# Macaron layer on one core: the last batch's scores in another order, first products drawn ahead, and the tile pools resized to make room

## The chip, the core and the metric

The kernel runs on one core of a Trainium2 chip. The metric is device time in microseconds (us). Its engines, as they are named here: PE (TensorE; PEld is its weight loading), DVE (VectorE), ACT (ScalarE), POOL (GpSimd) and SP (SyncE, which here only issues transfers). Each runs its own instructions in order, and they wait for each other by semaphores.

## The reference

`x` is 16 batches of 256 tokens of width 256, in float32. Three residual stages follow each other:

```
x = x + 0.5 * ffn(layernorm(x), w1, b1, w2, b2)     # w1, w2 quantised to -1, 0, 1
x = x + attn(layernorm(x), Wq, Wk, Wv, Wo)
x = x + 0.5 * ffn(layernorm(x), w1, b1, w2, b2)
# ffn:  gelu(x @ w1q.T + b1) @ w2q.T + b2, width 1024
# attn: 16 heads of 16, rotary embedding, causal softmax(q k / 4) v, then Wo
```

## The kernel before, in words

All 4096 tokens stay on the chip (`xs`, 8 tiles of 4 x 128 tokens). The two feed-forwards go over 8 blocks of 512 tokens, the attention over 16 batches of 256. Every instruction goes through the class `InOrder` (line 167, the line that the profile shows for nearly all of them), so each engine's order is the order of the Python calls.

**Feed-forward** (`ffn`, from line 273). A block's tokens are normalised into `xn` (`prepare`, line 282; one buffer), turned by PE and copied by ACT into `xnT` (`turn_in`, line 291; a high part and, by DVE's subtraction, a rest). `step(u)` (line 366) does for its block `i` and chunk `f` of 128 hidden columns: `up`, four PE products of 128x512 into a PSUM tile `m`, two GELUs on ACT (`h_high`, `h_whole`) and a subtraction (`h_rest`; on POOL for `f` 1, 3, 5, otherwise on DVE). Two steps later (`LATE = 2`, line 271) follows `down`: eight products into a tile `w` of `ps_w`. In step 3 of a block the next block is prepared, in steps 5 and 6 it is turned.

**Attention.** A batch passes through 8 places `p` of a slot (`slot(b, p)`, line 639). Each place computes two heads' transposed scores of batch `b-1` (tile `w`) and two heads' plain scores of batch `b` (two tiles `m`), PE's products of both kinds interleaved (`scores`, line 498). The plain scores serve for their row maxima alone: four times in a place DVE adds a mask and takes the negated maximum (lines 539 to 548). Such a call makes two instructions: `masked`, which writes a tile that nobody reads, and an accumulator read that writes the maximum. The tile `masked` is in pool `proj`, with 2 buffers. `turn_max` (line 487) turns the maxima of eight heads, and SP writes them into spare rows of `qT` with two transfers, so the later product subtracts them. `weigh` (line 550) adds the causal mask on DVE and takes the exponential on ACT into a tile `pT` (pool `probs`, 5 buffers). Around it, place by place, stand the other steps of neighbouring batches: `attend` (weights times values, copied to `avs`), `divide`, `turn_out`, `project_out`, `add_out`, `last_stats`.

PSUM is three pools of two tiles: `ps_w` (4 KB a partition, scores and down products), `ps_m`, and `ps_mm` for all else. A new tile waits until the last reader of its buffer is done; the scheduling layer puts in that wait, on the same engine too.

**The last turn** (lines 743 to 760). When slot 15 is over, only the last batch's transposed scores are left, 8 places without maxima. The steps of batches 13, 14 and 15 that remain (`a` = 14, `z` = 15) stand in the dictionaries `ahead` (between the scores and `weigh`) and `behind`. `project_out(13)` is in place 7 of slot 15 (line 668). Then the last feed-forward begins, with the tail of batch 15 after its first five steps (lines 761 to 771).

Of the kernel before, what the change touches and what calls it, by code (L numbers as in the profile page):

```python
# [8 lines left out]
FP = mybir.dt.float32  # L9
# [6 lines left out]
P = 128  # L16
# [6 lines left out]
S = 256  # L23
# [6 lines left out]
def kernel(  # L30
# [15 lines left out]
    NB = NT // S  # L46
# [8 lines left out]
    fp = ctx.enter_context(tc.tile_pool(name="ffn", bufs=2))  # L55
    pp = ctx.enter_context(tc.tile_pool(name="proj", bufs=2))
    hp = ctx.enter_context(tc.tile_pool(name="heads", bufs=2))
    prp = ctx.enter_context(tc.tile_pool(name="probs", bufs=5))

# [211 lines left out]
    def ffn(ln, after):  # L273
        xn, xnT, hT, ys = {}, {}, {}, {}

        def measure(i):
            if ln == 0:
                for t in range(BT):
                    stats(0, i * BT + t)
                finish_stats(0, i * BT, BT)  # L280

        def prepare(i, engine=None):
            xn[i] = fp.tile([P, BT, D], FP, name="xn", bufs=1)
            for t in range(BT):
                normalize(ln, i * BT + t, xn[i][:, t, :], engine)
            xnT[i] = [fp.tile([P, KC, TB], FR, name=f"xnT_{n}") for n in range(2)]

        def add_bias(i):
            gpsimd.tensor_add(xs[i], xs[i], b2_sb.unsqueeze(1).to_broadcast([P, BT, D]))

        def turn_in(i, k):
            tp = ps_mm.tile([P, TB], FP, name="mm")
            for t in range(BT):
                tensor.transpose(
                    tp[:, t * P : (t + 1) * P], xn[i][:, t, k * P : (k + 1) * P], ident
                )
            high, rest = (xnT[i][n][:, k, :] for n in range(2))
            scalar.copy(high, tp)
            return lambda: vector.tensor_sub(rest, tp, high.bitcast(FP))

        def up(i, f):
            h = ps_m.tile([P, TB], FP, name="m")
            for n in range(2):
                for k in range(KC):
                    tensor.matmul(
                        h,
                        w1q[:, k, f * P : (f + 1) * P],
                        xnT[i][n][:, k, :],
                        start=(n == 0 and k == 0),
                        stop=(n == 1 and k == KC - 1),  # L310
                    )
            high = fp.tile([P, TB], FR, name="h_high", bufs=LATE + 3)
            rest = fp.tile([P, TB], FR, name="h_rest", bufs=LATE + 3)
            whole = fp.tile([P, TB], FP, name="h_whole", bufs=3)
            scalar.activation(high, h, AF.Gelu, bias=b1_sb[:, f : f + 1])
            scalar.activation(whole, h, AF.Gelu, bias=b1_sb[:, f : f + 1])

            engine = gpsimd if f in (1, 3, 5) and not (ln == 0 and i == NBLK - 1) else vector
            engine.tensor_sub(rest, whole, high.bitcast(FP))
            hT[i, f] = (high, rest)  # L320

        def down(i, f):
            if f == 0 and ln == 2 and i == NBLK - 1:

                ys[i] = [ps_mm.tile([P, 2, D], FP, name="mm") for t in range(0, BT, 2)]
            elif f == 0:
                y = ps_w.tile([P, BT, D], FP, name="w")
                ys[i] = [y[:, t : t + 2, :] for t in range(0, BT, 2)]
            parts = hT.pop((i, f))
            order = [(t, n) for t in range(BT) for n in range(2)]  # L330
            if ln == 2 and (i, f) == (NBLK - 1, NFC - 1):

                order = [(t, n) for n in range(2) for t in range(BT)]
            for t, n in order:

                tensor.matmul(
                    ys[i][t // 2][:, t % 2, :],
                    parts[n][:, t * P : (t + 1) * P],
                    w2q[:, f, :],
                    start=(f == 0 and n == 0 and t % 2 == 0),  # L340
                    stop=(f == NFC - 1 and n == 1 and t % 2 == 1),
                )
            if f == NFC - 1:
                for t in range(0, BT, 2):
                    xt = xs[i][:, t : t + 2, :]
                    vector.scalar_tensor_tensor(
                        xt, ys[i][t // 2], 0.5, xt, ALU.mult, ALU.add
                    )
                for t in range(0, BT, 2):
                    after(i, t)  # L350

        def begin():
            measure(0)
            if ln == 0:
                sizes(0)
            prepare(0)
            if ln == 0:
                threshold(0)
                signs(0, lambda w: w[:, :, 0 : FF // 2])
            for k in range(KC):  # L360
                turn_in(0, k)()
            if ln == 0:
                signs(0, lambda w: w[:, :, FF // 2 :])
                sizes(1)

        def step(u):
            i, f = divmod(u, NFC)
            if i < NBLK:
                up(i, f)
                if ln == 0 and u == 0:  # L370
                    threshold(1)
                if ln == 0 and u in (0, 3):
                    part = slice(0, NFC // 2) if u == 0 else slice(NFC // 2, NFC)
                    signs(1, lambda w: w[:, part, :])
                if ln == 0 and u == 4:
                    gpsimd.tensor_scalar(b2_sb, b2_sb, 0.5, 0.0, ALU.mult, ALU.add)
                if u == 1:
                    measure(1)
                if ln == 0 and f >= 4 and i + 2 < NBLK:
                    stats(0, (i + 2) * BT + f - 4)  # L380
                    if f == NFC - 1:
                        finish_stats(0, (i + 2) * BT, BT)
                if i + 1 < NBLK:
                    if f == 3:
                        prepare(i + 1)
                    if f in (5, 6):
                        turn_in(i + 1, f - 5)()
                if f == (1 if i == NBLK - 1 else 6):
                    add_bias(i)
            if u >= LATE:  # L390
                down(*divmod(u - LATE, NFC))
            if ln == 0 and u == 2 * NFC + 2:
                make_tables()
            if ln == 0 and u < (NBLK - 1) * NFC and later:
                later.pop(0)()

        return begin, step, prepare, turn_in

    FFN_STEPS = NBLK * NFC + LATE

# [97 lines left out]
    def scores(bw, pw, bm, pm):  # L498
# [34 lines left out]
        if m is not None:  # L533
            for j in range(2):
                h = 2 * pm + j
                at = 32 * (h % 4) + HD * (1 - h // 4 % 2)
                for c in range(2):
                    cols = (c + 1) * P
                    vector.tensor_tensor_reduce(
                        out=pp.tile([P, S], FP, name="masked")[:, 0:cols],  # L540
                        in0=m[j][:, c * P : c * P + cols],
                        in1=mask_q[:, S - cols : S],
                        scale=-1.0,
                        scalar=-MASKED,
                        op0=ALU.add,
                        op1=ALU.min,
                        accum_out=maxes[bm % 2][:, c, h // 8, at : at + 1],
                    )
# [74 lines left out]
    def add_out(b):  # L623
        at = 2 * b % BT
        xt = xs[2 * b // BT][:, at : at + 2, :]
        vector.tensor_add(xt, y_a[b], xt)

    def last_stats(b):
        for c in range(2):
            stats(2, 2 * b + c)  # L630
        finish_stats(2, 2 * b, 2)
# [7 lines left out]
    def slot(b, p, more=lambda: None):  # L639
# [24 lines left out]
        if p == 6 and b + 2 < NB:  # L664
            turn_x(b + 2)
        if p == 7:
            if last is not None:
                project_out(last)
            if b + 3 < NB:
                ready_x(b + 3)  # L670
            if up is not None:
                spread(up, 0, 0)
# [57 lines left out]

    begin, step, prepare, turn_in = ffn(2, store)
    rest = []
    for p in range(8):
        made = []
# [4 lines left out]
        if p == 0:  # L741
            prepare(0, gpsimd)
    a, z = NB - 2, NB - 1
    add_out(NB - 3)
    ahead = {
        0: lambda: turn_max(z, 1),
        6: lambda: project_out(a),
    }
    behind = {
        0: lambda: attend(a, 1),  # L750
        4: lambda: turn_out(a),
        5: lambda: attend(z, 0),
        2: lambda: (divide(a, 1), last_stats(NB - 3)),
        7: lambda: (add_out(a), last_stats(a), divide(z, 0)),
    }
    for p in range(8):
        weigh = scores(z, p, None, None)
        ahead.get(p, lambda: None)()
        weigh()
        behind.get(p, lambda: None)()  # L760
    tail = [
        lambda: attend(z, 1),
        lambda: divide(z, 1),
        lambda: turn_out(z),
        lambda: project_out(z),
# [55 lines left out]
```

## Time and profile before

| | |
|---|---|
| median of 3 runs (range) | 623.16 us (622.33 to 626.79) |
| the profiled execution, its time | 622.22 us |
| its span | 620.4 us |
| TensorE clock granted | 1.00 |
| PE busy | 599.5 us, 97% of the span |
| DVE busy | 461.2 us, 74% |
| ACT busy | 416.3 us, 67% |
| POOL busy | 300.9 us, 49% |
| attention slots | about 163 to 466 us |
| last turn and the beginning of the last feed-forward | about 466 to 492 us |

The profile is of one execution. A group line gives line, engine, operation, tile written <- tiles read, shapes and count, then busy time and mean ns of one, then the engine's idle time just before them and what ended it. A timeline line gives start and length in us, engine, operation and, in brackets, the idle time before it and its releaser. Only idle time of the engine that sets the pace costs time.

### The profile page before, as it was taken

To read this page: it belongs to the slowest core of one execution; us is meant where nothing else is said; L and a number is where in the kernel's file an instruction comes from. 1 tells how busy PE (TensorE), PEld (TensorE's weight loads), DVE (VectorE), ACT (ScalarE), POOL (GpSimd) and SP (SyncE) were. 2 spreads that over 40 slices of the span, in tenths; PEclk is the share of its full clock that TensorE was granted. 3 is DMA by queue.
4 is the path that set the end of the run, shared out by engine and by line. 5 is a ranking of instruction groups with operands and counts; after the bars stand their busy time and mean duration, and the time that the engine had idled before them with its cause. 6 is when DMAs were issued, how large, how long until landed. Compare 5 with 4: busy or idle time off the path is not lost.

```text
span 620.4 us, 14716 instructions
## 1 busy us (share of the span) xinstructions
PE 599.5 (97%) x5580; PEld 486.6 (78%) x5580; DVE 461.2 (74%) x1654; ACT 416.3 (67%) x716; POOL 300.9 (49%) x273
## 2 busy tenths in 40 slices
PE   4999999999999999999999999999998999999997
PEld 3798999887667777777777777777766798888886
DVE  6877777786788888888888888888886465555553
ACT  4666766664576677676777677767765676676674
POOL 3655555782464455545564456453430243334443
PEclk9999999999999999999999999999999999999999
DMA  8800000000001000100001000100100011011001
GB/s 285 180 22 1 2 1 18 17 1 18 20 35 38 19 21 36 38 27 29 19 36 38 20 20 36 37 20 21 36 4 2 1 35 35 34 35 35 27 21 55
DMA packets 25478, 21.30 MB, mean 34 GB/s; under 512 B 10944, under 2 KB 21056, under 8 KB 25408
## 3 DMA queue, kind: packets, MB, share of 16 engines
q1 hardware_dynamic: 24848, 19.44, 9.8%
q8 instruction: 44, 0.72, 0.5%
q10 hardware_dynamic: 560, 0.92, 0.4%
q14 instruction: 26, 0.21, 0.1%
HBM read 7.51 MB, written 4.19 MB: 19 GB/s over the span
## 4 chain that ended last, share of the span: by engine, by line
PE 89%; DVE 5%; ACT 3%; issue 1%; DMA 1%; POOL 1%; DVEq 0%; SPq 0%; POOLq 0%
PE mm L167 38%; PE w L167 29%; PE m L167 22%; DMA w<-in_w1T_dram 1%; DVE h_rest L167 1%; DVE xn L167 1%; ACT h_high L167 1%; ACT h_whole L167 1%; DVE w2q L167 1%; DVE st L167 1%; DVE w L167 0%; DVE x L167 0%; DVE masked L167 0%; DVE mv L167 0%; ACT pT L167 0%
## 5 line engine op out<-in xcount | busy, mean ns | idle before, releaser
L167 DVE CUSTOM_DVE_ANT_0 masked<-m,mask_q 128x128 f32<-128x128 f32 x480 | 142.7, 354 | 41.0 <-PE m L167 39.7
L167 PE MATMUL m<-xnT,w1q 128*128 128x512 f32 x512 | 145.1, 404 | 0.8 <-ACT xnT L167 0.7
L167 ACT ACTIVATE h_high<-m,b_sb 128x512 fp32r<-128x512 f32 x128 | 88.5, 691 | 78.2 <-PE m L167 78.1
L167 DVE TENSOR_TENSOR h_rest<-h_whole,h_high 128x512 fp32r<-128x512 f32 x83 | 75.0, 904 | 72.0 <-ACT h_whole L167 71.5
L167 ACT ACTIVATE pT<-w 128x768 f32<-128x768 f32 x128 | 104.1, 815 | 31.4 <-DVE w L167 24.9
L167 PE MATMUL w<-qT,kT 32*128 32x256 f32 (+1 forms) x1024 | 120.6, 348 | 1.9 <-ACT pT L167 1.8
L167 PE MATMUL w<-w2q,h_high 128*128 128x256 f32 x480 | 120.8, 285 | 0.7 <-DVE w2q L167 0.7
L167 PE MATMUL w<-w2q,h_rest 128*128 128x256 f32 x480 | 117.8, 279 | 0.4 <-POOL h_rest L167 0.3
L167 PEld LDWEIGHTS w<-qT,kT 32*128 32x128 f32 x1024 | 89.9, 184 | 33.0 <-issue 25.9
L167 PE MATMUL m<-kT,qT 32*128 32x128 f32 x960 | 114.9, 349 | 0.7 <-ACT kT L167 0.7
L167 POOL TENSOR_TENSOR h_rest<-h_whole,h_high 128x512 fp32r<-128x512 f32 x45 | 60.1, 1335 | 108.5 <-ACT h_whole L167 108.4
L167 PEld LDWEIGHTS m<-xnT,w1q 128*128 128x128 f32 x512 | 88.3, 190 | 16.7 <-DVE xnT L167 2.9
L167 PEld LDWEIGHTS w<-w2q,h_rest 128*128 128x128 f32 x480 | 90.4, 188 | 5.1 <-POOL h_rest L167 0.7
L167 PEld LDWEIGHTS w<-w2q,h_high 128*128 128x128 f32 x480 | 90.3, 188 | 5.2 <-DVE w2q L167 1.2
L167 DVE TENSOR_TENSOR w<-w,mask_k 128x512 f32<-128x512 f32 x128 | 88.8, 695 | 7.1 <-PE w L167 7.0
L167 ACT ACTIVATE h_whole<-m,b_sb 128x512 f32<-128x512 f32 x128 | 87.3, 682 | 0.0
L167 PEld LDWEIGHTS m<-kT,qT 32*128 32x128 f32 x960 | 65.9, 185 | 2.9 <-ACT kT L167 1.6
L167 POOL TENSOR_TENSOR w<-w,cosT 128x512 f32<-128x512 f32 x32 | 41.3, 1292 | 51.8 <-ACT w L167 31.9
L167 PE MATMUL mm<-xnT_a,wqk 128*128 128x256 f32 x256 | 62.2, 386 | 0.0
L167 POOL TENSOR_SCALAR var<-mv 128x4 f32<-128x4 f32 (+1 forms) x32 | 6.9, 216 | 106.2 <-DVE mv L167 105.6
L167 POOL TENSOR_TENSOR w<-w,sinT 128x512 f32<-128x512 f32 x32 | 41.0, 1280 | 26.0 <-DMA w<-w 25.9
L167 PEld LDWEIGHTS mm<-xnT_a,wqk 128*128 128x128 f32 x256 | 46.1, 190 | 7.6 <-issue 0.7
(86 smaller groups left out, 918.9 us busy)
## 6 DMA issues: line engine op xcount, KB each, us to landing
w<-w SPq DMA_DIRECT2D x64, 128.0 KB
out_dram<-x SPq DMA_DIRECT2D x15, 256.0 KB
x<-in_x_dram SPq DMA_DIRECT2D x7, 512.0 KB
w<-in_w2T_dram SPq DMA_DIRECT2D x1, 1024.0 KB
qT<-mT SPq DMA_DIRECT2D x64, 4.0 KB
w<-in_w1T_dram SPq DMA_DIRECT2D x1, 512.0 KB
w<-in_w1T_dram ACTq DMA_DIRECT2D x1, 512.0 KB
wqk<-in_wqkvT_dram SPq DMA_DIRECT2D x16, 32.0 KB
```

Of the source, the lines that this page charges most:

```text
L167: return tc.keep_in_program_order(getattr(self.engine, name)(*args, **kwargs))
```

## The change

The last turn gets a new order, and work of the last feed-forward is put into it:

- `project_out(13)` leaves place 7 of slot 15 and stands in place 0 of the last turn; `turn_max(z, 1)` goes from place 0 to place 1, `attend(a, 1)` from 0 to 2, `divide(a, 1)` and `last_stats(13)` from 2 to 4, `turn_out(a)` from 4 to 5, `attend(z, 0)` from 5 to 6, `project_out(a)` from 6 to 7.
- `up` is split: `up_first` does the four PE products, and `up` uses a first product that is there already. Chunks 0 and 1 of block 0 are multiplied in places 3 and 5, into the two `m` tiles; chunks 2 and 3 after place 7, into one tile of `ps_w`.
- Block 1 of the last feed-forward is normalised on POOL in place 1 and turned in places 6 and 7, no longer in steps 3, 5 and 6.
- The tail has an empty entry after `attend(z, 1)`, so its later steps come one step later.
- Pool `probs` has 7 buffers instead of 5, the tile `masked` 1 instead of 2.

```diff
-    prp = ctx.enter_context(tc.tile_pool(name="probs", bufs=5))
+    prp = ctx.enter_context(tc.tile_pool(name="probs", bufs=7))
...
-        def up(i, f):
-            h = ps_m.tile([P, TB], FP, name="m")
+        first = {}
+
+        def up_first(i, f, to=None):
+            h = first[i, f] = ps_m.tile([P, TB], FP, name="m") if to is None else to
             for n in range(2):
                 for k in range(KC):
                     tensor.matmul(
...
+        def up(i, f):
+            if (i, f) not in first:
+                up_first(i, f)
+            h = first.pop((i, f))
             high = fp.tile([P, TB], FR, name="h_high", bufs=LATE + 3)
...
-                if i + 1 < NBLK:
+                if i + 1 < NBLK and (ln, i) != (2, 0):
                     if f == 3:
                         prepare(i + 1)
...
-                        out=pp.tile([P, S], FP, name="masked")[:, 0:cols],
+                        out=pp.tile([P, S], FP, name="masked", bufs=1)[:, 0:cols],
...
-            if last is not None:
+            if last is not None and b < NB - 1:
                 project_out(last)
...
-    add_out(NB - 3)
+
+
     ahead = {
-        0: lambda: turn_max(z, 1),
-        6: lambda: project_out(a),
+        0: lambda: project_out(NB - 3),
+        1: lambda: turn_max(z, 1),
     }
     behind = {
-        0: lambda: attend(a, 1),
-        4: lambda: turn_out(a),
-        5: lambda: attend(z, 0),
-        2: lambda: (divide(a, 1), last_stats(NB - 3)),
-        7: lambda: (add_out(a), last_stats(a), divide(z, 0)),
+        0: lambda: add_out(NB - 3),
+        1: lambda: prepare(1, gpsimd),
+        2: lambda: attend(a, 1),
+        3: lambda: up_first(0, 0),
+        4: lambda: (divide(a, 1), last_stats(NB - 3)),
+        5: lambda: (up_first(0, 1), turn_out(a)),
+        6: lambda: (turn_in(1, 0)(), attend(z, 0)),
+        7: lambda: (turn_in(1, 1)(), project_out(a), add_out(a), divide(z, 0), last_stats(a)),
     }
     for p in range(8):
         weigh = scores(z, p, None, None)
         ahead.get(p, lambda: None)()
         weigh()
         behind.get(p, lambda: None)()
+
+    more = ps_w.tile([P, 2, TB], FP, name="w")
+    for f in range(2):
+        up_first(0, 2 + f, more[:, f, :])
     tail = [
         lambda: attend(z, 1),
+        lambda: None,
         lambda: divide(z, 1),
```

More of the change, by code (lines that the diff above doesn't have):

```diff
@@ L395, in step @@
                 later.pop(0)()
-        return begin, step, prepare, turn_in
+        return begin, step, prepare, turn_in, up_first
     FFN_STEPS = NBLK * NFC + LATE
@@ L729, in store @@
             )
-    begin, step, prepare, turn_in = ffn(2, store)
+    begin, step, prepare, turn_in, up_first = ffn(2, store)
     rest = []
```

## The prediction

> **What bounds the kernel now.** I read the page first, then the timelines of DVE and PE in one attention slot and in the last turn, and last the order and the waits of both built programs.
>
> ```profile
> PE 599.5 (97%) x5580; PEld 486.6 (78%) x5580; DVE 461.2 (74%) x1654; ACT 416.3 (67%) x716; POOL 300.9 (49%) x273
> ...
> PE   4999999999999999999999999999998999999997
> ...
> DVE  6877777786788888888888888888886465555553
> ...
> L167 DVE CUSTOM_DVE_ANT_0 masked<-m,mask_q 128x128 f32<-128x128 f32 x480 | 142.7, 354 | 41.0 <-PE m L167 39.7
> ```
>
> PE is busy in 97% of the span; only at the start, the end and the slice of the last turn (digit 8) does it fall back. So PE is the bound, but in the attention slots (163 to 466 us) DVE runs at eight tenths beside it, and the largest DVE group there is `masked`, whose idle time is a wait for PE. By engine, over three stretches (a middle slot, slot 15, the last turn; columns: length, then PE, PEld, DVE, ACT, POOL busy):
>
> ```profile
> 324.30:344.50 20.20, 20.17 (x245) 15.54 (x244) 17.05 (x82) 14.33 (x27) 10.95 (x10) 1.00 0.08 29
> ...
> 445.30:466.30 21.00, 20.80 (x249) 14.45 (x248) 18.55 (x85) 14.62 (x27) 7.02 (x7) 1.00 0.01 3
> 466.30:490.10 23.80, 21.17 (x218) 15.81 (x219) 13.61 (x36) 14.72 (x22) 3.09 (x5) 1.00 0.01 2
> ```
>
> PE idles 23.80 - 21.17 = 2.63 us in the last turn. That is all a better order there can win: 0.4% of the span. The reader should set against it the 20.20 - 17.05 = 3.15 us of DVE slack in each slot, which the pool edit draws on.
>
> The edit that looks like bookkeeping is `masked` with one buffer for two. DVE's timeline in place 0 of a slot (start, length):
>
> ```profile
> 307.80 0.29 DVE L167 CUSTOM_DVE_ANT_0 masked<-m,mask_q 128x128 f32<-128x128 f32 x1
> 308.01 0.08 DVE L167 DVE_READ_ACCUMULATOR2_ANT maxes<- 128x1 f32 x1
> 308.01 0.42 DVE L167 CUSTOM_DVE_ANT_0 masked<-m,mask_q 128x256 f32<-128x256 f32 x1
> 308.36 0.08 DVE L167 DVE_READ_ACCUMULATOR2_ANT maxes<- 128x1 f32 x1
> ...
> 308.92 0.69 DVE L167 TENSOR_TENSOR w<-w,mask_k 128x512 f32<-128x512 f32 x1
> 309.52 0.42 DVE L167 BATCH_NORM_STATS2 st<-x 128x6 f32<-128x256 f32 x1
> 309.97 0.18 DVE L167 BATCH_NORM_AGGREGATE mv<-st 128x2 f32<-128x6 f32 x1
> 310.07 0.40 DVE L167 BATCH_NORM_STATS2 st<-x 128x6 f32<-128x256 f32 x1
> ```
>
> An instruction that waits for nothing on DVE starts about 0.08 before the end of the one ahead (second BATCH_NORM_STATS2: 310.07 against 309.97 + 0.18 = 310.15; second `masked`: 308.01 against 308.09). One that waits for the instruction just ahead starts 0.03 after its end (AGGREGATE: 309.97 against 309.94). So a wait for one's direct predecessor costs 0.03 + 0.08 = 0.12 us, unrounded 0.118.
>
> **The change part by part.**
>
> *`masked` with one buffer.* In the built program before, each `masked` waits for the accumulator read of the `masked` two back, long done. After, 387 of the 512 wait for the accumulator read directly ahead: three in each of the 128 places (the first has the mask addition between). Two of the three wait in the instruction itself: 2 x 0.118. The third (in 120 places) also waits for PE, so a separate semaphore instruction holds it; in the DVE timeline such an instruction at 306.94 is followed by its operation at 307.01, 0.07 later, so 0.118 to 0.18. Sum 0.354 to 0.416 per place; I take 0.38, between them.
>
> What hides it? DVE's idle time before a place's first `masked`, and PE's room: its next second `m` product starts some time after the last accumulator read that frees that bank, and needs 0.06 of it. One slot, 318 to 338 us, places 4,5,6,7,0,1,2,3: DVE idle 0.98, 0.49, 0, 0.55, 0.10 (and 0.19 before the `x` addition ahead of it), 0, 0.70, 0; room 0.10, 0.15, 0.16, 0.58, 0.10, 0.30, 0.16, 0.58 (place 4: the last read ends 319.42, PE's product starts 319.58). PE, never idle, cannot make up what it loses. Each step: DVE ends a place 0.38 later than it began late; PE's lateness in the next place is that less the room, or its own if greater; DVE begins at PE's lateness, or at its own less the idle time, whichever is greater. DVE ends late / next place's PE late: place 4: 0.38 / 0.28; 5: 0.66 / 0.51; 6: (begins 0.66) 1.04 / 0.88; 7: 1.26 / 0.88; 0: (begins 0.97) 1.35 / 1.25; 1: 1.73 / 1.43; 2: 1.81 / 1.65; 3: 2.19 / 1.65. So 1.65 us a slot. Although 8 x 0.38 = 3.0 is no more than DVE's slack, the slack lies in the wrong places. The same steps give 0.4 a slot at 0.18 per place, 1.5 at 0.354, 1.9 at 0.416, 2.9 at 0.54 (each wait at the dearest price).
> Slots 1 to 15 have both score sets: 15 x 1.65 = 24.8. Slot 0 has no `w` scores and long feed-forward work between its first places; from place 4 on PE follows the last read by 0.06, so some two and a half places pay in full: 1.0.
>
> The Trainium skill speaks against this: "VectorE: DVE Perf Modes", section "The DRAIN you can't avoid", says that the next operation cannot start before the pipe is empty anyway, and that a semaphore between chained operations cost nothing extra when measured. By that rule this term is 0 and the sum is 623.1. The rows above differ by 0.118 between waiting and not waiting, and I go by them.
>
> *Probabilities with 7 buffers.* No instruction is added; `attend(a,1)` two places later needs the two tiles. 0.
>
> *The last turn.* PE's matrix products are the same. Place 0 of it now starts at 466.54, where `project_out(13)` (1.92) started, which covers place 0's way through DVE (0.70) and ACT (0.81). One `w` buffer turns round in 2.7 to 2.8 us (place 5: scores 476.64, exponential ends 479.29). With the work now between, places start at 0, 2.8, 4.0, 6.4, 8.2, 9.4, 11.6, 14.3, each 3.0 or more after the place before last. So the waits for `pT` shown here go:
>
> ```profile
> 473.76 1.62 PE L167 MATMUL w<-qT,kT 32*128 32x256 f32 x16 [1.10 <-ACT pT L167]
> ...
> 476.64 0.92 PE L167 MATMUL w<-qT,kT 32*128 32x256 f32 x8 [0.68 <-ACT pT L167]
> ...
> 487.41 0.66 PE L167 MATMUL mm<-ident,avs 128*128 128x128 f32 x4 [0.58 <-ACT avs L167]
> ```
>
> What is late next: ACT. All four first products are spent before the first GELU, and ACT can begin that only behind the last exponential, block 1's second copy (0.59) and the table load (1.28 at 484.31). Counted on from place 7 (scores end 15.1): its mask addition follows a copy and a subtraction, the exponential ends 17.1, the copy 17.7, the load 19.0, GELU pair 0 20.2. `turn_in(1,1)` waits 0.45 for a `mm` bank (the copy of `avs` ends 15.5); `divide(z,0)` waits 0.65 for the subtraction (18.4). `avs` of `attend(z,1)` ends 22.8, pair 1 24.05, POOL's `h_rest` (1.29) 25.4: the second down product waits there from 23.4, 2.0. That is 3.1 of new idle for 2.63 of old: +0.5. Places 1 and 2 ran side by side before (471.12: 16 products in 0.95, against 0.86 for 8 alone) and no longer do: +0.8. So +1.3; counted on to the same finished work (less the 0.7 of block 1's turning, already done) I get +0.4 only. I take the middle, +0.9. Bounds: -2.6 (all idle gone) to +2.3: SP's two transfers of `qT` are issued one place later and place 4 follows 3.4 us after the copy of the maxima, not 4.4, so up to 1.0 on top is unseen.
> Block 1's `prepare` moves from DVE (4 x 0.35, off the path) to POOL: 4 x 1.22 = 4.9, inside POOL's idle 17 us; behind it only `var` of batch 13 queues, needed much later. Uncovered, it would hold `turn_in(1,0)`, at place 6. 0.
>
> *Sum.* Span 620.4 + 24.8 + 1.0 + 0.9 = 647.1; the profiled execution took 622.22, 1.82 more than its span: 648.9. It lies 0.94 below the median of the runs (623.16).
>
> **The rivals.**
> - *The wait is hidden* (the other side). DVE's 3.15 us of slack a slot speaks for it, the rooms of 0.10 to 0.16 in five of eight places against it. It decides where the extra per place stays below 0.10, some 0.03 a wait. Then the turn alone is left: 623.1, from 619.6 to 624.5.
> - *The wait is half as dear* (0.06 each, 0.18 a place): 15 x 0.4 + 0.5 + 0.9 = 7.4: 629.6. For it: the accumulator read is a short instruction that no row here shows being waited for.
> - *DVE becomes the bound throughout*: every place pays in full, 128 x 0.38 = 48.6: 671. Against it: idle of 0.5 to 1.0 in four of eight places.
> - *The new turn does not do what it says*: the feed-forward runs dry behind the table load. I hold this likely already; it is worth 2 us at most.
>
> **How the numbers follow.** Forecast (630 to 662) 0.80; half price or between (625 to 630) 0.07; hidden (619 to 625) 0.09; above 662 0.04. The range, 8 in 10, is 630 to 662: 0.18 a place below, 0.50 above. A measurement of this kernel tells about 1% (6.2 us) from no change: 629.4 is the line. Faster by over 1% would need 616.9, more than all PE idle of the turn: 0.02. Same 0.13, slower 0.85.
>
> **What would show it.** Right: starts of consecutive `masked` 0.33, 0.46 and 0.33 to 0.39 apart instead of 0.21, 0.35, 0.21; a slot of 21.9 instead of 20.2; waits of PEld `m` for DVE `maxes` of tens of us; PE below 97%. In the turn: no wait for `pT`, one near 2 us for POOL `h_rest`. Wrong: gaps of `masked` unchanged, or wider gaps with slots of 20.2 (the slack did hide them), or a longer wait in the turn for `qT` or the table load.

## The result, and the profile after

The changed kernel takes 654.3 us (median of 6 runs, 653.52 to 657.53); the kernel before took 623.99 us in the same comparison (6 runs, 622.26 to 626.79). The ratio is 1.0495, its 95% interval 1.0466 to 1.0525: slower by 5%. Runs of the kernel before differ in the mean granted clock (0.990 to 1.00), so its median moves between 624.0 and 626.9 from one comparison below to the next; where a difference of a microsecond matters, spans of profiled executions are compared instead.

The page of after (busy time and share by engine; three groups):

```profile
span 651.7 us, 14718 instructions
...
PE 629.1 (97%) x5580; PEld 494.1 (76%) x5580; DVE 491.2 (75%) x1650; ACT 421.6 (65%) x716; POOL 306.0 (47%) x277
...
L167 DVE CUSTOM_DVE_ANT_0 masked<-m,mask_q 128x128 f32<-128x128 f32 x480 | 171.1, 356 | 42.7 <-PE m L167 15.2
...
L167 PE MATMUL m<-kT,qT 32*128 32x128 f32 x960 | 139.4, 356 | 2.3 <-DVE maxes L167 1.5
...
L167 PEld LDWEIGHTS m<-kT,qT 32*128 32x128 f32 x960 | 84.5, 185 | 11.2 <-DVE maxes L167 7.4
```

The plain scores of PE (the group in the middle) on the page of before:

```profile
L167 PE MATMUL m<-kT,qT 32*128 32x128 f32 x960 | 114.9, 349 | 0.7 <-ACT kT L167 0.7
```

One `masked` takes the same mean time (356 ns against 354), and the group's busy time is 28 us longer: the calls overlap less (480 times 354 ns is 170 us, of which only 142.7 counted as busy before). PE executes the same 5580 instructions and is "busy" 30 us longer, 24.5 of it in the 960 plain scores, whose mean hardly grew (349 to 356 ns): they too are spread out. So no share tells of the loss: PE still reads 97%. The ends of PE's products are modelled, and much of the time in which DVE holds PE is booked as busy. One has to measure the distance between the same two events instead.

The slot that began at 307.80 before and lasted 20.24 us begins here at 322.69 and lasts 21.96; slot 15 follows (columns as shown in the prediction; before, then after):

```profile
307.80:328.04 20.24, 20.21 (x248) 15.56 (x252) 17.09 (x81) 14.37 (x27) 10.95 (x10) 1.00 0.08 28
449.39:466.54 17.15, 16.71 (x209) 11.36 (x209) 15.38 (x73) 11.69 (x22) 5.75 (x6) 1.00 0.01 3
```

```profile
322.69:344.65 21.96, 21.93 (x248) 15.91 (x252) 19.08 (x81) 14.81 (x27) 10.94 (x10) 1.00 0.07 26
...
476.61:496.49 19.88, 18.57 (x208) 12.00 (x207) 17.44 (x75) 12.67 (x23) 8.11 (x8) 1.00 0.01 3
```

DVE's timeline of place 0 of that slot, to be laid beside the one of before:

```profile
322.69 0.29 DVE L167 CUSTOM_DVE_ANT_0 masked<-m,mask_q 128x128 f32<-128x128 f32 x1
322.91 0.09 DVE L167 DVE_READ_ACCUMULATOR2_ANT maxes<- 128x1 f32 x1
323.03 0.42 DVE L167 CUSTOM_DVE_ANT_0 masked<-m,mask_q 128x256 f32<-128x256 f32 x1
323.38 0.08 DVE L167 DVE_READ_ACCUMULATOR2_ANT maxes<- 128x1 f32 x1
323.61 0.29 DVE L167 CUSTOM_DVE_ANT_0 masked<-m,mask_q 128x128 f32<-128x128 f32 x1
...
323.94 0.42 DVE L167 CUSTOM_DVE_ANT_0 masked<-m,mask_q 128x256 f32<-128x256 f32 x1
```

The starts of the four `masked` are 0.33, 0.58 and 0.33 apart; before they were 0.22, 0.34 and 0.21. No instruction is longer. Each `masked` now begins only after the read ahead of it has ended, and the third stands off furthest.

Where the 31.3 us of span went (651.7 - 620.4), by the start of each slot's first `masked` and of PE's first work of the last turn (`project_out(13)` before, place 0's scores after):

| stretch | before | after | longer by |
|---|---|---|---|
| up to the end of slot 0 | 0 to 165.02 | 0 to 166.36 | 1.34 |
| slots 1 to 14 | 165.02 to 449.39 | 166.36 to 476.61 | 25.88 |
| slot 15 | 449.39 to 466.54 | 476.61 to 496.49 | 2.73 |
| last turn to the end | 466.54 to 620.4 | 496.49 to 651.7 | 1.35 |

Most middle slots lose 1.7; slots 1 to 3, 6 and 7 lose about 2. Slot 15 loses 2.73. Of that, 0.24 belongs to the new turn, whose first scores wait for `pT` (below): the same stretch is 17.39 in the kernel with the new turn and two buffers for `masked`, the second experiment, against 17.15 before. The other 2.5 (19.63 with the pool edit alone) are more than a middle slot loses; slot 15 has less PE work (16.71 us busy before, against 20.21), so probably less to hide behind.

The three waits that PE has left in the turn (start, length, in brackets the idle time and its releaser):

```profile
496.49 0.92 PE L167 MATMUL w<-qT,kT 32*128 32x256 f32 x8 [0.54 <-ACT pT L167]
...
515.50 0.66 PE L167 MATMUL mm<-ident,avs 128*128 128x128 f32 x4 [0.59 <-DVE xnT L167]
...
522.73 0.39 PE L167 MATMUL w<-w2q,h_rest 128*128 128x256 f32 x1 [1.54 <-POOL h_rest L167]
```

The waits of 1.10, 0.68 and 0.58 of before are gone. In their place stand `pT` ahead of the first scores, the subtraction that makes `xnT`, half a microsecond ahead of the first GELU (516.04), and POOL's `h_rest` behind it.

### The profile page after: what moved, and what is told of

It is laid out like the page before. It is cut to its first block, busy times and chain, and to the rows that moved or that the text cites. A ratio compares the mean times of both kernels' runs of the same rounds, so it can differ in the third digit from the quotient of the medians.

```text
span 651.7 us, 14718 instructions
## 1 busy us (share of the span) xinstructions
PE 629.1 (97%) x5580; PEld 494.1 (76%) x5580; DVE 491.2 (75%) x1650; ACT 421.6 (65%) x716; POOL 306.0 (47%) x277
## 4 chain that ended last, share of the span: by engine, by line
PE 86%; DVE 8%; ACT 2%; issue 1%; DMA 1%; POOL 1%; DVEq 0%; SPq 0%; ACTq 0%; POOLq 0%
PE mm L167 34%; PE w L167 27%; PE m L167 25%; DVE masked L167 3%; DMA w<-in_w1T_dram 1%; DVE h_rest L167 1%; DVE xn L167 1%; ACT h_high L167 1%; DVE st L167 1%; ACT h_whole L167 1%; DVE w2q L167 1%; DVE w L167 0%; DVE x L167 0%; POOL h_rest L167 0%; DVE mv L167 0%
## 5 line engine op out<-in xcount | busy, mean ns | idle before, releaser
L167 DVE CUSTOM_DVE_ANT_0 masked<-m,mask_q 128x128 f32<-128x128 f32 x480 | 171.1, 356 | 42.7 <-PE m L167 15.2
L167 PE MATMUL m<-xnT,w1q 128*128 128x512 f32 x504 | 143.5, 406 | 0.8 <-ACT xnT L167 0.8
L167 PE MATMUL m<-kT,qT 32*128 32x128 f32 x960 | 139.4, 356 | 2.3 <-DVE maxes L167 1.5
L167 ACT ACTIVATE h_high<-m,b_sb 128x512 fp32r<-128x512 f32 x126 | 86.7, 688 | 77.7 <-PE m L167 77.5
L167 PE MATMUL w<-qT,kT 32*128 32x256 f32 (+1 forms) x1024 | 125.3, 352 | 0.8 <-ACT pT L167 0.5
L167 PEld LDWEIGHTS m<-kT,qT 32*128 32x128 f32 x960 | 84.5, 185 | 11.2 <-DVE maxes L167 7.4
L167 ACT ACTIVATE h_whole<-m,b_sb 128x512 f32<-128x512 f32 x126 | 85.8, 681 | 0.0
```

The lines of the kernel that those rows point to most:

```text
L167: return tc.keep_in_program_order(getattr(self.engine, name)(*args, **kwargs))
```

## The experiments

**The pool edit alone.** The kernel before, with one buffer for `masked` and nothing else.

```diff
-                        out=pp.tile([P, S], FP, name="masked")[:, 0:cols],
+                        out=pp.tile([P, S], FP, name="masked", bufs=1)[:, 0:cols],
```

> The kernel before with one edit: the tile masked has one buffer instead of two; last turn and probability pool as before. Theory (the wait of each masked for the read directly ahead): the whole loss of the slots is here. The changed kernel's first score product of the last turn starts 29.95 us later than the work in its place did before (496.49 against 466.54), so 622.2 + 30 = 652, 650 to 654, starts of consecutive masked 0.33, 0.58, 0.33 apart and a slot of 22.0 us. Rival (the new order or the larger probability pool makes most of the loss): under 640.

Measured: 655.9 us (4 runs, 654.62 to 660.55), ratio 1.0495 (1.045 to 1.0539). One slot of it:

```profile
325.50:347.46 21.96, 21.93 (x248) 15.91 (x252) 19.07 (x81) 14.80 (x27) 10.93 (x10) 1.00 0.07 26
```

The same slot length as in after, and the same gaps of 0.33, 0.58 and 0.33. This one line makes the loss of the slots, all but some 1.5 us of the whole; those come from the new turn, as the next experiment shows.

**Everything but that.** The kernel after, with two buffers again; the tile that nobody reads is now bfloat16, and two of it take the room of one in float32.

```diff
-                        out=pp.tile([P, S], FP, name="masked", bufs=1)[:, 0:cols],
+                        out=pp.tile([P, S], mybir.dt.bfloat16, name="masked")[:, 0:cols],
```

> The changed kernel with the unread tile masked in bfloat16 and two buffers, which take the room of the one float32 buffer; the maxima are still accumulated in float32. Everything else as changed. Theory: the waits go back to the read two masked ahead, the gaps to 0.21, 0.35, 0.21, the slots to 20.2 us, and only the new last turn is left: +1.35 us by the distance from its first score product to the end (155.2 against 153.9), so 623.6, 622 to 626. Rival (the new order slows the slots too, by memory places or the deeper pool): 630 or more.

Measured: 623.79 us (11 runs, 623.61 to 624.16), ratio 0.9972 (0.9955 to 0.9989), span 621.9. DVE's timeline:

```profile
307.73 0.29 DVE L167 CUSTOM_DVE_ANT_0 masked<-m,mask_q 128x128 bf16<-128x128 f32 x1
307.94 0.08 DVE L167 DVE_READ_ACCUMULATOR2_ANT maxes<- 128x1 f32 x1
307.94 0.42 DVE L167 CUSTOM_DVE_ANT_0 masked<-m,mask_q 128x256 bf16<-128x256 f32 x1
```

The second `masked` starts with the read again, not 0.12 behind its start, and slots last 20.24. The calls themselves last as long as in float32 (0.29 and 0.42), so the shorter type alone makes none faster. By spans the kernel with the new turn alone is then 1.5 us longer than before (621.9 against 620.4), where the prediction had 0.9. That the median is nevertheless a little lower goes with the clock; the last section comes back to it.

**Waits taken singly.** Three kernels, each the kernel before with several `masked` tiles of one buffer, so that only some of the three waits remain: the second and fourth (in the instruction itself), the third alone (held by a separate semaphore instruction), the fourth alone.

```diff
-                        out=pp.tile([P, S], FP, name="masked")[:, 0:cols],
+                        out=pp.tile([P, S], FP, name=f"masked_{j}", bufs=1)[:, 0:cols],                       # second and fourth
+                        out=pp.tile([P, S], FP, name=f"masked_{j ^ c}", bufs=1)[:, 0:cols],                   # third
+                        out=pp.tile([P, S], FP, name=f"masked_{c if j == 0 else 2}", bufs=1)[:, 0:cols],      # fourth
```

> The kernel before with masked split into one buffer per head of the place: the second and the fourth masked of a place wait for the read directly ahead, in the instruction itself; the third does not. Measured prices in the changed kernel: 0.33 - 0.215 = 0.115 each, 0.23 a place. Theory (the slack of the places takes part of it, the steps of the prediction): at 0.23 a place some 0.63 us a slot, 15 slots and about 0.6 in slot 0: +10 us, 629 to 636. Rival (every wait costs in proportion to its length, 0.23 of 0.47 a place of 29 us): +14.5, 636 to 639. Second rival (all of it is hidden below some threshold): within 2 us of before.

> The kernel before with two buffers for masked that alternate so that only the third masked of a place waits for the read directly ahead; it also waits for PE, so a separate semaphore instruction holds it. Measured price in the changed kernel: 0.58 - 0.345 = 0.235 a place. Theory (slack and prediction's steps): the same +10 us as with the second and fourth waits, 629 to 636, and a gap of 0.58 between the second and the third masked alone. Rival (in proportion): +14.5. Rival (the separate semaphore instruction costs only behind another wait): gap near 0.46, under +5 us.

> The kernel before with three tiles for masked, shared so that only the fourth masked of a place waits for the read directly ahead: 0.115 us a place. Theory (the rooms of 0.10 to 0.16 take the first tenth of a microsecond of a place): by the prediction's steps 0.1 us a slot, 1.5 to 2 in all, within 1% of before, the slots 20.3 us. Rival (every wait costs in proportion, 0.115 of 0.47 a place of 30 us): +7.4, 1.2% slower, the slots 20.7.

| waits | gaps of `masked` | extra a place | slot | median us (runs) | ratio (95%) |
|---|---|---|---|---|---|
| none (before) | 0.22, 0.34, 0.21 | 0 | 20.24 | 624.48 (35) beside the fourth, 625.4 (15) beside the others | 1 |
| fourth | 0.22, 0.34, 0.33 | 0.12 | 20.33 | 625.99 (12) | 1.0034 (1.0012 to 1.0056) |
| second, fourth | 0.33, 0.35, 0.33 | 0.23 | 20.78 | 633.08 (4) | 1.0127 (1.009 to 1.0164) |
| third | 0.22, 0.57, 0.22 | 0.23 | 20.73 | 632.37 (4) | 1.0123 (1.0083 to 1.0163) |
| all three (the pool edit alone) | 0.33, 0.58, 0.33 | 0.47 | 21.96 | 655.9 (4) | 1.0495 (1.045 to 1.0539) |

The ratios also carry differences in clock between the runs. In runs with a mean clock of 0.998 or more the spans are 620.2 to 620.5 before (one 621.1), 622.8 to 623.0 with the fourth wait, 630.5 and 630.7 with the second and fourth, 630.4 to 630.6 with the third: 2.5, 10 and 10 us more. The two tens are as expected, the 2.5 is a little above.

The third wait alone, in DVE's timeline:

```profile
321.12 0.42 DVE L167 CUSTOM_DVE_ANT_0 masked<-m,mask_q 128x256 f32<-128x256 f32 x1
321.47 0.08 DVE L167 DVE_READ_ACCUMULATOR2_ANT maxes<- 128x1 f32 x1
321.69 0.29 DVE L167 CUSTOM_DVE_ANT_0 masked<-m,mask_q 128x128 f32<-128x128 f32 x1
```

The read ends at 321.55 and the third `masked` starts 0.14 later, where a wait in the instruction itself ends after 0.03. The two halves of 0.23 a place cost 0.5 a slot each; together they cost 1.7. The first 0.12 is nearly free: a slot pays 0.09, where eight places of 0.12 add up to 0.96. From 0.23 to 0.47 a slot pays some 1.2 of 1.9. That is what slack looks like, and it rules out a cost that is proportional to the number of waits, as it rules out both the hidden and the everywhere-in-full rival.

**Mending the new turn.** Five further kernels start from the one with two bfloat16 buffers and move only steps around the last turn.

```diff
     tail = [
-        lambda: attend(z, 1),
         lambda: None,
+        lambda: attend(z, 1),
         lambda: divide(z, 1),
```

> The changed kernel with two short buffers for masked (as in the run of that name) and the empty entry of the tail put first, so that ACT makes the second GELU pair before the copy of avs of the last attend and not after it. In the changed kernel ACT stood idle 2.28 us ahead of that copy, and PE then waited 1.54 us for POOL's h_rest of the second pair. Theory (the turn's loss is that order on ACT): the wait goes, the span falls by some 1.5 us to 620.4. Rival (PE waits somewhere else next, for the copy of avs): span 621.5 or more.

Measured: 622.52 us (12 runs), ratio 0.9979 (0.9961 to 0.9997), span 620.6. The wait for POOL's `h_rest` is gone; ACT takes GELU pair 1 directly behind pair 0. A wait of 0.55 for `o` comes at `turn_out` (492.85). The span fell by 1.3, about as expected.

```diff
-        7: lambda: (turn_in(1, 1)(), project_out(a), add_out(a), divide(z, 0), last_stats(a)),
+        7: lambda: (turn_in(1, 1)(), project_out(a), add_out(a), two_more(), divide(z, 0), last_stats(a)),
```

Here `two_more` holds the first products of chunks 2 and 3, which stood behind the loop.

> The same, and the third and fourth first products put ahead of the division of the last batch's first half in PE's order. In the changed kernel PE waited 0.59 us at that division for DVE's subtraction. Theory: the wait is covered by 1.9 us of products, the span falls by 0.6 to 619.8. Rival (the products themselves wait for the exponential of place 6, or the division's result is late for the next step): no gain against the run with the empty entry first.

Measured: 622.66 us (12 runs), ratio 0.9973 (0.9955 to 0.9991), span 620.8. PE's waits after place 0:

```profile
489.81 0.38 PE L167 MATMUL w<-w2q,h_rest 128*128 128x256 f32 x1 [0.71 <-DVE h_rest L167]
491.89 0.38 PE L167 MATMUL w<-w2q,h_rest 128*128 128x256 f32 x1 [0.42 <-POOL h_rest L167]
```

The 0.59 for `xnT` is covered and the 0.55 for `o` is gone, and 1.13 appears in their place: nothing gained, against the 0.6 expected.

A third kernel in addition put `project_out(13)` back into place 7 of slot 15, and places 1 to 5 one earlier.

> The same, and the projection of batch 13 back in place 7 of slot 15, with the steps of places 1 to 5 one place earlier; so the first score product of the turn, which waited 0.54 us for an exponential, stands behind that projection. Theory: another 0.5 us, span 619.3, 0.2 to 0.4% under the kernel before. Rival (the wait returns at places 2 or 4, since a w buffer turns round in 2.7 us): span 619.8 or more.

Measured: 622.62 us (12 runs), ratio 0.9977 (0.9962 to 0.9993), span 621.0. The 0.54 for `pT` becomes 0.28 for `xnT` at 466.62; the waits of 0.71 and 0.42 stay. No gain, and the 0.5 us expected did not come; the waits that the rival foresaw at places 2 or 4 did not come back either, so why nothing was gained stays open.

The 0.71 is a wait for DVE, on which `last_stats(a)` stands ahead of `h_rest`. The 0.42 is a wait for POOL, but it hangs on the same statistics: POOL works on their `var` and `rstd` from 489.28 to 490.59 and starts its own `h_rest` only at 490.56. The last step moves `last_stats(a)` out of place 7; POOL's `h_rest` then starts at 488.75:

```diff
-        7: lambda: (turn_in(1, 1)(), project_out(a), add_out(a), two_more(), divide(z, 0), last_stats(a)),
+        7: lambda: (turn_in(1, 1)(), project_out(a), add_out(a), two_more(), divide(z, 0)),
...
-        lambda: divide(z, 1),
+        lambda: (divide(z, 1), last_stats(a)),
```

> The run with the products ahead of the division, with last_stats of batch 14 moved from place 7 into the tail behind the last division, so that DVE subtracts the first h_rest before those four statistics. There PE waited 0.71 us for DVE's h_rest and 0.42 for POOL's. Theory (DVE's order made the first of these waits): it goes or halves, the span falls by some 0.5 to 1 us to 620. Rival (the table load sets it: whatever is taken away, the first products run out before the GELU pairs are ready): the wait moves on to POOL's h_rest and the span stays at 620.5 or more.

> The same on top of the run with the projection of batch 13 back in slot 15. Theory: span 620.0, 0.3% under the kernel before. Rival: 620.7 or more, no better than the run with the empty entry first.

Measured: 621.8 us (6 runs, 621.69 to 622.1), ratio 0.9933 (0.9913 to 0.9953), span 619.9; with `project_out(13)` back in slot 15 622.07 us, ratio 0.9937 (0.9915 to 0.9959), span 620.0. In the first, only two waits are left:

```profile
466.78 0.92 PE L167 MATMUL w<-qT,kT 32*128 32x256 f32 x8 [0.54 <-ACT pT L167]
492.13 0.44 PE L167 MATMUL mm<-ident,o 128*128 128x128 f32 x2 [0.54 <-DVE o L167]
```

By its median this version is 0.7% under the kernel before, but most of that goes with the clock: in runs with a mean clock of 0.998 or more the spans are 619.9 to 620.3 (six runs) against 620.2 to 620.5 before (one 621.1). So the reordered turn, with most of its waits mended, is itself worth a few tenths of a microsecond.

## Why the prediction held, step by step

- **A wait for the direct predecessor costs 0.118.** Right for the second and fourth `masked`: gaps grew by 0.11 to 0.12. The rule of the Trainium skill weighed there ("VectorE: DVE Perf Modes", section "The DRAIN you can't avoid"), by which the sum would have been 623.1, does not hold for these instructions: the pool edit alone cost 4.95%, and the two waits of that kind alone 1.27%.
- **The third wait costs 0.118 to 0.18.** Failed. This is the term that was mis-sized: it costs 0.23 to 0.24, so a place pays 0.47, not 0.38. The prediction took the separate semaphore instruction's price from the one ahead of the `x` addition (0.07 from it to its operation). Ahead of the third `masked` that distance is 0.10 to 0.11, and the semaphore instruction itself starts 0.04 behind the read, so 0.14 pass from the read's end to the operation. Why the distance is longer here than ahead of the addition was not tried and stays open. In slot 0 the third `masked` waits for DVE alone, no separate instruction is there, and the gap is 0.47 in after too (142.01 to 142.48), not 0.58.
- **The recursion over the places gives 1.65 a slot.** The measure is 1.72 in most slots, but that the number fits is luck: two errors cancel. With 0.47 a place the same steps would give 2.3. How much later each place's first `masked` starts in after than in before, counted from place 4 of the slot shown above to place 4 of the next:

| place | 4 | 5 | 6 | 7 | 0 | 1 | 2 | 3 | 4 |
|---|---|---|---|---|---|---|---|---|---|
| predicted, 0.38 a place | 0 | 0.28 | 0.66 | 0.88 | 0.97 | 1.35 | 1.43 | 1.81 | 1.65 |
| the same steps, 0.47 a place | 0 | 0.37 | 0.84 | 1.15 | 1.33 | 1.80 | 1.97 | 2.44 | 2.33 |
| measured | 0 | 0.17 | 0.64 | 0.75 | 0.95 | 1.43 | 1.40 | 1.86 | 1.72 |

  The shape is the predicted one, place by place, so the mechanism holds; its steps are too strict at "DVE begins at PE's lateness". After and before at the start of place 5 (the first product into each of the two `m` tiles, the banks of the prediction, then the first `masked`):

```profile
335.25 0.37 PE L167 MATMUL m<-kT,qT 32*128 32x128 f32 x1
...
335.62 0.49 PE L167 MATMUL m<-kT,qT 32*128 32x128 f32 x2
...
336.37 0.29 DVE L167 CUSTOM_DVE_ANT_0 masked<-m,mask_q 128x128 f32<-128x128 f32 x1 [0.19 <-PE m L167]
```

```profile
319.57 0.37 PE L167 MATMUL m<-kT,qT 32*128 32x128 f32 x1
319.58 0.48 PE L167 MATMUL m<-kT,qT 32*128 32x128 f32 x3
...
320.53 0.29 DVE L167 CUSTOM_DVE_ANT_0 masked<-m,mask_q 128x128 f32<-128x128 f32 x1 [0.49 <-PE m L167]
```

  Before, both banks' products start together, and the first `masked` 0.96 later. After, the second bank is held until the last read of the place before, 0.37 behind the first; the first `masked` needs only the first bank and starts 1.12 behind that. Of the 0.37 only 0.16 reaches DVE; the rest is taken up by the two tiles, which are freed one after the other. That the slack is used up place by place, which was the core of the argument, fits the steps of the table of single waits too: 0.09, 0.5 and 1.7 a slot for 0.12, 0.23 and 0.47 a place. For the fourth alone the recursion's size was right (0.1 against 0.09), for 0.23 it was a little high (0.66 against 0.54 and 0.49).
- **15 such slots, 24.8; slot 0, 1.0.** They came to 28.6 and 1.34. Slot 15 was counted as an ordinary one but has less PE work and lost 2.5 by the waits, 2.73 with the new turn's 0.24; slots 1 to 3, 6 and 7 lost about 2. At the start of slot 1 the clock was lower, 0.71 between 165 and 170 us, which may be its part; for the others, at a clock of 1.00, it stays open.
- **The last turn, +0.9.** +1.35 in after, and +1.3 over the same stretch in the kernel with two buffers; with the 0.24 that fell into slot 15 the turn cost some 1.5, inside the bounds. The waits: 0.59 for the subtraction (0.65 predicted), 1.54 for POOL's `h_rest` (2.0 predicted). The 0.45 for an `mm` bank did not appear, and neither did any wait for `qT`. The 0.54 for `pT` ahead of the turn was not foreseen; place 0's scores need a `w` buffer, and `project_out(13)` had covered that wait while it stood ahead of them. All named waits of PE together are as long as before (2.67 against 2.64 us, with 0.28 ahead of `project_out(13)` before), so the loss is not in named waits; the prediction had 0.8 for places 1 and 2, which no longer run side by side, and no run takes that part singly.
- **The sum.** Span 651.7 against 647.1: the slots made 3.8 of the difference, the turn and slot 0 0.8.
- **The signs.** The slot came as described, and so did the first and the last gap. The middle one, ahead of the third `masked`, was to be 0.46 and was 0.58; the prediction had also put the range for the dearer wait at the last gap, though by its own sum it belongs to the middle one. Two signs did not come, though the mechanism was right: PE's share stayed 97%, and named waits for `maxes` came to 7.4 us, not tens. The lost time lies inside PE's modelled busy time, so both were poor signs.
- **The rivals.** Hidden: refuted by the pool edit alone. Half price: refuted by the gaps. DVE the bound throughout: 128 x 0.47 = 60 would have been the loss, half of it came. The new turn that runs dry behind the table load: a wait of 1.54 for `h_rest` came, small as foreseen, but the load did not set it. It went when the tail's empty entry came first, and in the last version no wait for `h_rest` is left with the load (1.28 us) in the same place.

## What to carry to other kernels

A scratch tile that nobody reads still orders its writers: with one buffer, each waits for the one ahead, and on DVE that broke an overlap of 0.08 us and added 0.03, or 0.14 where the instruction also waited for another engine. Cut the type of such a tile before its number of buffers. Slack per slot says little about what a fixed cost in every place does: add it place by place, because the first 0.12 a place was nearly free here (0.09 of 0.96 a slot) and the last 0.24 was not (1.2 of 1.9).

## What the runs showed of the hardware

**The second wait of an instruction.** On DVE, ahead of a `masked`, a wait carried by a separate semaphore instruction costs 0.11 to 0.12 more than the same wait in the instruction itself when it is the one that ends last (gaps 0.57 to 0.58 in 119 places of after, against 0.47 in the 8 of slot 0). Raw start and end in after: read to 323.462, semaphore instruction 323.500 to 323.521, `masked` from 323.606.

**The clock behind the old turn.** PE's granted clock can drop behind the old turn, without a long wait of PE. The kernel that waits for the second and fourth, behind its last slot (length; PE, PEld, DVE, ACT, POOL busy; clock):

```profile
480.00:485.00 5.00, 3.90 (x64) 3.03 (x56) 2.97 (x10) 2.91 (x4) 0.00 (x0) 1.00 0.02 5
485.00:490.00 5.00, 4.35 (x40) 2.78 (x40) 1.81 (x3) 2.46 (x4) 0.91 (x2) 0.56 0.00 0
490.00:495.00 5.00, 5.00 (x26) 3.56 (x19) 0.70 (x1) 1.74 (x3) 0.00 (x0) 0.50 0.00 0
```

The kernel that waits for the third shows the same at the same place (0.64, then 0.50). The same five microseconds of before, in the execution shown, had no drop behind them:

```profile
470.00:475.00 5.00, 3.90 (x65) 2.99 (x59) 2.94 (x9) 3.08 (x5) 0.00 (x0) 1.00 0.02 5
475.00:480.00 5.00, 4.32 (x59) 3.08 (x56) 2.07 (x5) 3.28 (x5) 0.91 (x2) 1.00 0.00 0
```

So the same order of work drops the clock to half for about 10 us in one execution and not in another. Runs of the kernel before go from 622.2 us at a mean clock of 1.00 to 627 at 0.990; that the slower ones drop at this place is likely, but no trace of one shows it. Of the 61 runs of before in the comparisons of the experiments 12 had a mean clock of 0.998 or more; of the 59 runs of the six kernels with the new turn and two buffers 54 had, and the 11 runs of the first of these scatter by less than 0.6 us. By the medians this steadier clock is most of what those kernels gain. The new turn does not keep it up everywhere: after itself ran at 0.991 to 1.00, with the drop at 165 us.

A short stretch of less work is not enough for a drop. In the kernel with the new turn and two buffers PE waited 1.53 us, was busy for 3.46 of five, and kept its clock, as it did in the next five:

```profile
490.00:495.00 5.00, 3.46 (x26) 3.05 (x25) 1.29 (x3) 4.27 (x8) 2.39 (x2) 1.00 0.00 0
```

The Trainium skill ("TensorE: Matmul & The Clock Gate", section "What's actually happening") gives half clock after an idle window of about 3.4 us and says that the window runs freely. The half clock agrees, and a free-running window would fit that it strikes only some runs; but no wait of PE near the drops shown was longer than about 1.1 us, so a rule that forbids only gaps over 3.4 us would not have warned here. What trips it was not tried and stays open.
